# Two Mamba layers: GpSimd's products moved to slots 2, 7 and 12 of a block, the gates and some background steps one slot later

## The chip, the cores and the metric

The kernel runs on one core of one Trainium2 chip. The core's engines each work through their own list of instructions in order and wait for each other by semaphores: TensorE (PE, with PEld for its weight loads), VectorE (DVE), ScalarE (ACT), GpSimd (POOL) and SyncE (SP, which here issues the DMAs). The metric is the device time of one launch in microseconds (us). The kernel before takes 11773.98 us, the median of three runs (11769.27 to 11785.81).

## The reference, cut to what matters

Four images of 256 channels by 64 x 64 pixels go through four residual layers: two of gated recurrence with windowed attention, one Mamba layer, one grouped Mamba layer. The change is in the last two. Both hold the same selective scan, over 4096 tokens; the Mamba layer has 512 inner channels, the grouped one has four groups of 64 channels with 128 inner channels each:

```python
def step(h, inp):
    d_t, u_t, B_t, C_t = inp
    dA = jnp.exp(d_t[..., None] * A)
    h = dA * h + (d_t * u_t)[..., None] * B_t[:, None, :]
    y_t = jnp.einsum('bdn,bn->bd', h, C_t)
    return (h, y_t)
_, ys = jax.lax.scan(step, h0, xs)
y = ys.transpose(1, 0, 2) + u * D
y = y * jax.nn.silu(z)
```

The state has 16 columns n for each channel. `B` and `C` are rows per token that all channels share; `delta` (`d_t`) and `u` are per channel and token. In the grouped layer the result goes on through a layer norm, two dense layers with a gelu, a 1x1 convolution and a batch norm.

## The kernel before, in words

Each layer cuts the tokens into four chunks of 1024 (`k`), and each chunk into four blocks of 128 channels (in the grouped layer a block is a group; a chunk has two pairs `c`, and a pair has an even and an odd block). `scan_blocks` (L907 to L1072) runs all 16 blocks of a layer in one list of 256 slots: one slot is one state column n of one block, so a block has slots 0 to 15. In slot i:

- TensorE spreads row n of B over 128 partitions into a PSUM tile `pb` (`spread`, L949), VectorE multiplies it by `du` (delta times u; L1029), ScalarE computes `da` = exp(delta A) (`decay`, L961), VectorE scans (L1039).
- GpSimd multiplies the scanned `h` by the row of C, `cb`, which a DMA has spread (L925), giving `hc` (L1045). TensorE transposes `hc` and adds it up in `y` (`turn`, L977), one slot behind.
- Slots named in the argument `apart` do the product with B otherwise: a DMA spreads the row of B into `bb` (L931), GpSimd multiplies it by `du` (`product`, L935) two slots ahead of its scan, and VectorE only scans. There `da` is kept in the PSUM tile in place of `pb` and is called `dap`. The first slot of a layer is never apart.

The order of every engine is written out by hand in the loop:

```python
for i, (blk, n) in enumerate(slots):
    if not is_apart(i): nc.vector.tensor_tensor(pb[i], blk["du"], pb[i], ALU.mult)
    for step in blk["bg"].get(("between", n), ()): step()
    if i >= DS: gate(slots[i - DS][0], n)
    ...                       # VectorE's scan of slot i
    product(i + 2)
    ...                       # GpSimd's hc of slot i
    decay(i + 3); keep(i - 1); load_c(i + 3); load_b(i + 4)
    ...                       # the block before: end(); background steps of slot n
    spread(i + 2)
    ...                       # background steps of slot n + 0.5
    turn(i - 1); decay(i + 2, True)
```

`pb` and `dap` share two PSUM buffers (so slot i + 2 can be filled once scan i is done), `h`, `hc` have three buffers, `cb` four, `bb` one, `y` one. The block before is finished while the next one runs: in the slots of `ends` ScalarE copies `y` out (L995) and TensorE turns it back in two halves (L1001); in the slots of `gates` VectorE multiplies the two halves by the silu of z, ahead of that slot's scan (L988).

All other work is background: `put(block, slots, steps)` hangs the steps of the next chunk or pair onto slots. A step ("between", n) goes ahead of the scan of slot n, a step n behind the `hc` of slot n, a step n.5 behind the `spread`. The steps that this document follows: `norm` (position and add on GpSimd in the Mamba layer, mean L1103, center L1106, deviation L1117 to L1081, scale L1123 on GpSimd, affine L1130), `x_proj` (two projections whose results go by DMA to the tables of B and C, then the three bf16 parts of B, with the two `rest` products on GpSimd, L1206), `delta` (two projections, two additions on VectorE L1171, and `du` on GpSimd L1175), `mlp` (its scaling L1815 is on GpSimd), and `out` (an addition on GpSimd L1896 and a DMA out).

Of the kernel before, what the change touches and what calls it, by code (L numbers as in the profile page):

```python
# [28 lines left out]
NC = 1024  # L29
# [15 lines left out]
class Net:  # L45
# [1191 lines left out]
    def mamba_layer(self, x, bridge, pe_dram, w_in, w_cw, w_x, w_dt, w_out, v_dram):  # L1237
        tc, nc = self.tc, self.nc
        ND = 4
        with ExitStack() as ctx:  # L1240
            wp = ctx.enter_context(tc.tile_pool(name="m2_w", bufs=1, reuse_waits="tile"))
            work = ctx.enter_context(tc.tile_pool(name="m2_a", bufs=2, reuse_waits="tile"))
            loop = ctx.enter_context(tc.tile_pool(name="m2_b", bufs=2, reuse_waits="tile"))
            dram = ctx.enter_context(tc.tile_pool(name="m2_d", bufs=2, space=DRAM))
            psum = ctx.enter_context(tc.tile_pool(name="m2_p", bufs=2, space=PSUM))
            psb = ctx.enter_context(tc.tile_pool(name="m2_q", bufs=2, space=PSUM))
# [243 lines left out]
            for k in range(n_chunk):  # L1490
                more = k + 1 < n_chunk
                bg = [blk["bg"] for blk in chunks[k]["blocks"]]

                def put(d, where, steps):
                    for i, f in zip(where, steps):
                        bg[d].setdefault(i, []).append(f)

                def soft(d, places, steps):
                    p0, a0, p1, a1, du = places
                    put(d, (p0, ("between", a0), p1, ("between", a1), du), steps)  # L1500

                if k == 0:
                    put(0, (2, 3, 4, 5), [lambda d=d: diag_taps(d) for d in range(ND)])
                if k:
                    for i, where in enumerate(((3, 4, 5), (6, 7, 8), (9, 10, 11), (12, 13, 14))):
                        put(0, where, out_proj(k - 1, i // 2, i % 2))
                soft(0, (9, 11, 11, 13, 13), delta(k, 1))
                put(0, (14, 15), (in_z(k, 0, 0), in_z(k, 0, 1)))
                z1 = in_z(k, 1, 0), in_z(k, 1, 1)
                z3 = in_z(k, 3, 0), in_z(k, 3, 1)  # L1510
                put(1, (0, 1, 2, 4), (*z1, *z3))
                put(1, (1.5,), (silu((k, 0, "zs"), (k, 1, "zs")),))
                soft(1, (6, 8, 8, 11, 11), delta(k, 2))
                at = (6, 8, 8, 10, 10) if more else (5, 7, 7, 9, 9)
                soft(2, at, delta(k, 3))
                at = (10, 11) if more else (8, 9)
                put(2, at, (in_z(k, 2, 0), in_z(k, 2, 1)))
                if more:

                    if k == 0:  # L1520
                        put(0, (0,), (lambda: begin(1),))
                        put(0, (0, 0, 1, 3, 4, 5, 6, 7), self.later(lambda: norm(1, 0), 8))
                    h1 = self.later(lambda k=k: norm(k + 1, 1), 8)
                    if k:
                        put(0, (2, 4, 5, 7, ("between", 9), 13, 14, 15), h1)
                    else:
                        put(0, (7, 8, 9, 12, ("between", 14), 14, 15), h1[:7])
                        put(1, (1,), h1[7:])
                    if k + 2 < n_chunk:
                        put(3, (3,), (lambda k=k: begin(k + 2),))  # L1530
                        h0 = self.later(lambda k=k: norm(k + 2, 0), 8)
                        put(3, (4, 6, 7, 14, 15), h0[:5])
                        chunks[k + 1]["late"] = ((0, 1, 2), h0[5:])
                    if k:
                        put(0, *chunks[k]["late"])
                    u = all_u(k + 1)
                    put(1, (5, 7, 9, 10, 11, 12, 13, 14, 15), u[:9])
                    put(2, (0, 1, 5, 7, 9, 12, 13, 14, 15), u[9:18])
                    put(3, (0, 1, 2, 4, 5, 6), u[18:])
                    xs = x_proj(k + 1)  # L1540
                    put(2, (13,), (silu((k + 1, 0, "u"), (k + 1, 1, "u"), (k, 2, "zs"),
                                        (k, 3, "zs")),))
                    put(3, (7,), (silu((k + 1, 2, "u"), (k + 1, 3, "u")),))
                    put(3, (8, 8.5, 9, 9.5), xs)
                    soft(3, (10, 12, 11, 13, 13), delta(k + 1, 0))
                    put(3, (10, 11, 12, 13), xs[4:])
                else:
                    put(2, (13,), (silu((k, 2, "zs"), (k, 3, "zs")),))

                    sums, about, square, squares, early_squares = stats  # L1550

                    def square_into(i):
                        tag, bufs = ("pe", 1) if i % 2 else ("u", 5)
                        square(i, work.tile([P, NC], F32, tag=tag, name="cs_sq", bufs=bufs))

                    for i in range(6):
                        put(1 + (13 + i) // DS, ((13 + i) % DS,), (lambda i=i: sums(i),))
                        put(2 + (12 + i) // DS, ((12 + i) % DS,), (lambda i=i: square_into(i),))
                        put(2 + (13 + i) // DS, ((13 + i) % DS,), (lambda i=i: squares(i),))
                    put(2, (3,), (about,))  # L1560
                    put(3, (3,), (early_squares,))
                    for i in range(4):
                        at = (6 + 2 * i, 7 + 2 * i)
                        put(3, at, out_proj(k, i // 2, i % 2, ((0, 1, 2),)))
# [18 lines left out]
            def center(s):  # L1583
# [5 lines left out]
                )  # L1589

            self.scan_blocks(
                [blk for c in chunks for blk in c["blocks"]], loop, psum, psb, psy, (0, 5, 10),
                (1, 2, 4), (3, 5), (xs0[4:6], (), xs0[6:]),
                {1: [lambda: mean3(0)], 2: [lambda: center(0)], 4: [lambda: mean3(1)],
                 5: [lambda: center(1)]},
            )
# [52 lines left out]
    def grouped_mamba_layer(self, x, bridge, begun, ws_dram, outc_dram, v_dram, out_b, load):  # L1649
        tc, nc = self.tc, self.nc  # L1650
        w_in, w_cw, w_x, w_dt, w_out, w_f1, w_f2 = ws_dram
        with ExitStack() as ctx:
# [123 lines left out]
            def x_proj(k, q):  # L1776
                blk = chunks[k]["blocks"][q]

                def make():
                    blk["bct"] = work.tile([P, NC], F32, tag="bct", name="m3_bct", bufs=1)  # L1780
                    blk["parts"] = work.tile([P, NC], BF16, tag="parts", name="m3_parts")
                    blk["cd"] = dram.tile([2, DS, NC], F32, tag="cd", name="m3_cd")

                def project(ps, ss, part):
                    nc.tensor.matmul(ps, wx, blk["u"][:, ss], start=True, stop=True)

                return self.table_steps(blk, make, project, psum, 1)

            def delta(k, q):
                return self.delta_steps(chunks[k]["blocks"][q], wdt, work, psum)  # L1790
# [101 lines left out]
            def out(k, s, m, eng=nc.gpsimd):  # L1892
                def step():
                    t0 = k * NC + s
                    xs = x[:, m * T + t0 : m * T + t0 + NT]
                    eng.tensor_tensor(yo(k, s, m), xs, yo(k, s, m), ALU.add)  # L1896
                    nc.sync.dma_start(out_b[m * P : (m + 1) * P, t0 : t0 + NT], yo(k, s, m))

                return step
# [110 lines left out]
            for i, (k, c) in enumerate(pairs):  # L2010
                even, odd = chunks[k]["blocks"][2 * c : 2 * c + 2]

                def put(blk, where, steps):
                    for i, f in zip(where, steps):
                        blk["bg"].setdefault(i, []).append(f)

                def soft(blk, places, steps):
                    p0, a0, p1, a1, du = places
                    put(blk, (p0, ("between", a0), p1, ("between", a1), du), steps)
# [7 lines left out]
                if more:  # L2027
                    h0, h1 = (self.later(lambda k=k, s=s: norm(k + 1, s), 5) for s in range(2))
                    put(even, (0,), (lambda k=k: begin(k + 1),))
                    put(even, (0, ("between", 2), 4, 5, 6), h0)  # L2030
                    put(even, (14, 15), h1)
                    put(odd, (1, 2, 3), h1[2:])
                put(even, (4, 5, 9, 11, 12, 13) if i else (6, 7, 9, 11, 12, 13), x_proj(k, 2 * c + 1))
                if i:
                    m0, m1 = mlp(*pairs[i - 1], 0), mlp(*pairs[i - 1], 1)
                    put(even, (6, 7, 8, 10, 11, 11.5, 12.5, 13.5), m0)
# [6 lines left out]
                        late.append(((0, 0.5, 1.5, 2), m1[4:]))  # L2043
                    else:
                        put(odd, (5, 6, 6.5, 7.5, 8.5), m1[3:])
                soft(even, (7, 9, 8, 10, 10) if i else (9, 11, 10, 12, 12), delta(k, 2 * c + 1))
                also = [lambda k=k: out_silu(k - 1)] if c == 1 and k else []
                if i == 0:
                    put(even, (1, 2), [in_z(0, 0, s) for s in range(2)])
# [4 lines left out]
                    put(even, (12, 13, 14, 15), folds)  # L2054
                put(even, (3 if i else 5,), (silu(k, c, "zs", also),))
                if c == 1 and k:
                    put(even, (4, 5, 6, 7), [out(k - 1, *sm) for sm in outs])
                    put(even, (8,), [lambda k=k: load(slice((k - 1) * NC, k * NC))])
                if c == 0 and k:
                    put(odd, (8, 12, 15), [out_conv(k - 1, *sm) for sm in outs[:3]])  # L2060
                    late.append(((0,), [out_conv(k - 1, *outs[3])]))
# [6 lines left out]
                    soft(odd, (10, 12, 11, 13, 13), delta(nk, 2 * ncol))  # L2068
                    put(odd, (13, 14), [in_z(nk, ncol, s) for s in range(2)])
            self.scan_blocks(  # L2070
                [blk for c in chunks for blk in c["blocks"]], loop, psum, psb, psy, (0, 4, 8),
                (1, 2, 3), (3, 4), (xs0[2:4], (), xs0[4:]),
            )

            k, pair = n_chunk - 1, chunks[-1]["blocks"][2:]
# [160 lines left out]
```

## Time and profile before

| what | value |
|---|---|
| median of three runs | 11773.98 us |
| the profiled execution | 11766.22 us, span 11764.4 us |
| scan stages of the Mamba layer, four images | 927.3, 927.2, 925.7, 927.7 us |
| scan stages of the grouped layer, four images | 956.5, 955.6, 956.9, 954.5 us |
| the eight scan stages together | 7531.3 us, 64% of the span |
| VectorE busy in a scan stage | about 869 us (both layers) |
| GpSimd busy in a scan stage | about 799 us (Mamba), 852 us (grouped) |
| ScalarE busy in a scan stage | about 537 us (Mamba), 678 us (grouped) |
| TensorE busy in a scan stage | about 750 us (Mamba), 745 us (grouped), clock granted 0.94, 0.91 |

A scan stage is counted from the first scan's start to the last scan's end in the trace. The four images run alike, to within 2 us. Busy time is the sum of an engine's instructions; what is left of a stage is time in which that engine waited for something.

### The profile page before, as it was taken

The page shows a single profiled execution, that of the slowest core. Times are in us where ns is not written, and L with a number is a line of the kernel's source. Part 1 is how long each engine was busy: PE and PEld are TensorE (multiplying, and loading weights), DVE is VectorE, ACT ScalarE, POOL GpSimd, SP SyncE. Part 2 cuts the span into 40 slices and gives each one's busy share as a digit, 9 for nine tenths or more (in the row PEclk, how much of TensorE's full clock was granted, in tenths as well). Part 3 has the DMA queues.
Part 4 walks back from the last instruction along what each step waited for, and adds up shares of the span by engine and source line. Part 5 has one row for each costly group of instructions (what it writes and reads, how often), then busy time and mean ns, then how long its engine had stood idle before and what let it go on. Part 6 is the DMA issues. An engine that isn't in the chain of part 4 may idle for free. (4 is left out here: it accounts for less than half of the span.)

```text
span 11764.4 us, 192822 instructions
## 1 busy us (share of the span) xinstructions
PE 9808.9 (83%) x71200; PEld 5732.9 (49%) x71200; DVE 9739.8 (83%) x8290; ACT 7203.5 (61%) x13520; POOL 8779.1 (75%) x6054
## 2 busy tenths in 40 slices
PE   8997887777899788777799978877778997887787
PEld 4564444444466444444446644444444564444444
DVE  6677998898667799889866779988987678998898
ACT  4566555776456655577645665557764566555776
POOL 4666887898466688789846668878984666887897
PEclk9998998999999899899999999989999999998999
DMA  3344544454334454445423445544543344554454
GB/s 98 105 138 139 177 171 150 167 179 163 88 107 137 138 176 174 148 169 180 165 83 111 139 141 177 174 148 168 180 161 92 104 141 147 171 176 150 168 172 154
DMA packets 682477, 1742.10 MB, mean 148 GB/s; under 512 B 88880, under 2 KB 194880, under 8 KB 681280
## 3 DMA queue, kind: packets, MB, share of 16 engines
q1 hardware_dynamic: 676416, 1721.38, 44.5%
q8 instruction: 564, 9.24, 0.3%
q10 hardware_dynamic: 5120, 8.39, 0.3%
q14 instruction: 377, 3.09, 0.1%
HBM read 1601.49 MB, written 94.39 MB: 144 GB/s over the span
## 5 line engine op out<-in xcount | busy, mean ns | idle before, releaser
L1045 POOL TENSOR_TENSOR hc<-h,cb 128x1024 f32<-128x1024 f32 x2056 | 4810.6, 2351 | 792.1 <-DVE h L1039 403.6
L1039 DVE TENSOR_TENSOR_SCAN h<-da,m_state,pb 128x1024 f32<-128x1024 f32 x1248 | 2917.7, 2338 | 144.6 <-ACT m_state L966 17.8
L977 PE MATMUL y<-ident,hc 128*128 128x128 f32 x16384 | 2380.5, 293 | 518.9 <-POOL hc L1045 404.4
L977 PEld LDWEIGHTS y<-ident,hc 128*128 128x128 f32 x16384 | 2053.8, 151 | 1271.3 <-POOL hc L1045 691.8
L1029 DVE TENSOR_TENSOR pb<-du,pb 128x1024 f32<-128x1024 f32 x1672 | 2020.4, 1208 | 140.7 <-PE pb L949 134.7
L961 ACT ACTIVATE da<-delta,m_v 128x1024 f32<-128x1024 f32 x1672 | 1898.2, 1140 | 136.3 <-DVE h L1039 110.0
L949 PE MATMUL pb<-m_parts,pick 128*128 128x512 bf16 x3312 | 1076.3, 409 | 929.7 <-DVE h L1039 886.2
L603 POOL TENSOR_SCALAR pr<-pr,sm,zero 128x256 f32<-128x256 f32 x2048 | 1107.3, 556 | 375.2 <-DVE sm L600 371.0
L588 ACT ACTIVATE pr<-sc,mn 128x256 f32<-128x256 f32 x2048 | 953.0, 477 | 507.2 <-DVE sm L600 400.7
L949 PEld LDWEIGHTS <-pick 128*128 128x128 bf16 x3312 | 258.7, 101 | 1823.0 <-DVE h L1039 1196.6
L577 DVE TENSOR_REDUCE mn<-sc 128x4 f32<-128x1024 f32 x512 | 630.1, 1232 | 529.5 <-PE sc L565 529.5
L1039 DVE TENSOR_TENSOR_SCAN h<-da,pb 128x1024 f32<-128x1024 f32 x424 | 968.4, 2284 | 54.5 <-ACT m_state L966 11.3
L935 POOL TENSOR_TENSOR bb<-du,bb 128x1024 f32<-128x1024 f32 x376 | 888.2, 2362 | 127.4 <-DMA bb<-m_cd 113.3
L1039 DVE TENSOR_TENSOR_SCAN h<-dap,m_state,bb 128x1024 f32<-128x1024 f32 x288 | 673.5, 2338 | 95.0 <-POOL bb L935 67.8
L252 PE MATMUL conv_ps<-att_y,att_wb 128*128 128x512 f32 x1536 | 682.5, 594 | 0.0
L616 PE MATMUL pt_ps<-ident,pr 128*128 128x128 f32 x4096 | 638.0, 291 | 41.3 <-POOL pr L603 20.8
L961 ACT ACTIVATE dap<-delta,m_v 128x1024 f32<-128x1024 f32 x376 | 418.6, 1113 | 338.5 <-DVE h L1039 323.3
L565 PE MATMUL sc<-kv,q_swap 32*64 32x128 f32 x8192 | 592.8, 282 | 18.9 <-DMA kv<-kv_dram 8.0
L565 PE MATMUL sc<-kv,att_y 32*64 32x128 f32 x7168 | 573.3, 282 | 23.6 <-DMA kv<-kv_dram 20.5
L616 PEld LDWEIGHTS pt_ps<-ident,pr 128*128 128x128 f32 x4096 | 458.8, 146 | 169.6 <-POOL pr L603 111.9
L290 DVE SCALAR_TENSOR_TENSOR lp<-vimg,att_v,lp 128x512 f32<-128x512 f32 x672 | 507.7, 755 | 30.4 <-DVE lp L290 0.5
L565 PEld LDWEIGHTS sc<-kv,att_y 32*64 32x64 f32 x7168 | 424.9, 136 | 154.2 <-ACT pr L588 72.6
(303 smaller groups left out, 17725.3 us busy)
## 6 DMA issues: line engine op xcount, KB each, us to landing
cb<-m_cd SPq DMA_DIRECT2D x2048, 512.0 KB, 3.8
kv<-kv_dram SPq DMA_DIRECT2D x1984, 128.0 KB, 2.8
bb<-m_cd SPq DMA_DIRECT2D x376, 512.0 KB, 4.9
kv_dram<-kst SPq DMA_DIRECT2D x128, 256.0 KB, 3.6
kv_dram<-vn SPq DMA_DIRECT2D x128, 256.0 KB, 4.1
q_swap<-att_y SPq DMA_DIRECT2D x96, 256.0 KB, 4.3
m_pe<-in_pe_dram SPq DMA_DIRECT2D x32, 512.0 KB, 4.3
out_dram<-yo SPq DMA_DIRECT2D x64, 256.0 KB, 2.4
```

Of the source, the lines that this page charges most:

```text
L252: nc.tensor.matmul(ps, w[:, k, w0 + m * P : w0 + (m + 1) * P], src[:, k], start=(k == 0), stop=(k == 1),)
L565: nc.tensor.matmul(sc[h][b * 64 : b * 64 + 64, r, w, m, :], (own(sj, m) if r == b else swap[sj % 2][:, m])[rows, 2 * a + w], kv[i, w][rows ...
L588: nc.scalar.activation(t[:, g].rearrange("p j r t -> p r j t"), sc[h][:, :, g // 2, g % 2, :].rearrange("p r (j t) -> p r j t", j=2), AF.E ...
L603: nc.gpsimd.tensor_scalar(t[:, g], t[:, g], s[:, g : g + 1], self.zero, ALU.mult, ALU.add)
L616: nc.tensor.transpose(pt[h][j][:, g, :], t[:, g, j].rearrange("p r t -> p (r t)"), self.ident,)
L935: nc.gpsimd.tensor_tensor(pb[i], slots[i][0]["du"], pb[i], ALU.mult)
L949: nc.tensor.matmul(pb[i][:, ss], self.pick[:, n : n + 1].to_broadcast([P, P]), blk["parts"][:, ss], start=True, stop=True,)
L961: nc.scalar.activation(da[i], blk["delta"], AF.Exp, scale=blk["a"](n))
L977: nc.tensor.matmul(blk["y"][:, ss], t[:, ss], self.ident, is_transpose=True, start=(n == 0 and ss.start % NT == 0), stop=(n == DS - 1 and ...
L1029: nc.vector.tensor_tensor(pb[i], blk["du"], pb[i], ALU.mult)
L1039: nc.vector.tensor_tensor_scan(h[i][:, ss], da[i][:, ss], pb[i][:, ss], state, ALU.mult, ALU.add)
L1045: nc.gpsimd.tensor_tensor(hc[i][:, ss], h[i][:, ss], cb[i][:, ss], ALU.mult)
```

## The change

In `scan_blocks`'s arguments, `apart` becomes (2, 7, 12) in both layers (it was (0, 5, 10) in the Mamba layer and (0, 4, 8) in the grouped one), and both gates of a block move one slot later. In the Mamba layer three steps of the second norm of a chunk move one slot later (add, mean, center). In the grouped layer the even block's norm of the next chunk's first half, the first two steps of `x_proj`, the second addition of `delta` with `du`, the four additions to the output with their DMAs, and the load of the next image's columns move one slot later.

```diff
 mamba_layer
-                        put(0, (2, 4, 5, 7, ("between", 9), 13, 14, 15), h1)
+                        put(0, (2, 4, 6, 8, ("between", 10), 13, 14, 15), h1)
...
-                ... loop, psum, psb, psy, (0, 5, 10), (1, 2, 4), (3, 5), ...
+                ... loop, psum, psb, psy, (2, 7, 12), (1, 2, 4), (4, 6), ...
 grouped_mamba_layer
-                    put(even, (0, ("between", 2), 4, 5, 6), h0)
+                    put(even, (1, ("between", 3), 4, 6, 7), h0)
...
-                put(even, (4, 5, 9, 11, 12, 13) if i else (6, 7, 9, 11, 12, 13), x_proj(k, 2 * c + 1))
+                put(even, (5, 6, 9, 11, 12, 13) if i else (6, 7, 9, 11, 12, 13), x_proj(k, 2 * c + 1))
...
-                soft(even, (7, 9, 8, 10, 10) if i else (9, 11, 10, 12, 12), delta(k, 2 * c + 1))
+                soft(even, (7, 9, 8, 11, 11) if i else (9, 11, 10, 12, 12), delta(k, 2 * c + 1))
...
-                    put(even, (4, 5, 6, 7), [out(k - 1, *sm) for sm in outs])
-                    put(even, (8,), [lambda k=k: load(slice((k - 1) * NC, k * NC))])
+                    put(even, (5, 6, 7, 8), [out(k - 1, *sm) for sm in outs])
+                    put(even, (9,), [lambda k=k: load(slice((k - 1) * NC, k * NC))])
...
-                ... loop, psum, psb, psy, (0, 4, 8), (1, 2, 3), (3, 4), ...
+                ... loop, psum, psb, psy, (2, 7, 12), (1, 2, 3), (4, 5), ...
```

## The prediction

> **What bounds the kernel now.** I read the page's groups first, then VectorE's waits, then its timeline slot by slot.
>
> ```profile
> span 11764.4 us, 192822 instructions
> ...
> L1045 POOL TENSOR_TENSOR hc<-h,cb 128x1024 f32<-128x1024 f32 x2056 | 4810.6, 2351 | 792.1 <-DVE h L1039 403.6
> L1039 DVE TENSOR_TENSOR_SCAN h<-da,m_state,pb 128x1024 f32<-128x1024 f32 x1248 | 2917.7, 2338 | 144.6 <-ACT m_state L966 17.8
> ...
> L1029 DVE TENSOR_TENSOR pb<-du,pb 128x1024 f32<-128x1024 f32 x1672 | 2020.4, 1208 | 140.7 <-PE pb L949 134.7
> ...
> L935 POOL TENSOR_TENSOR bb<-du,bb 128x1024 f32<-128x1024 f32 x376 | 888.2, 2362 | 127.4 <-DMA bb<-m_cd 113.3
> ```
>
> The last number before the bar is the count, then busy us and mean ns, then the idle time ahead. A normal slot costs VectorE 1.21 + 2.34, 3.6 us with the gaps; an apart slot 2.26. A block needs 13 x 3.6 + 3 x 2.26 = 53.6 us plus gates, additions and centers, while GpSimd's fixed part is 19 x 2.36 = 44.8 us. VectorE is busy about 869 us in each stage of 926 to 957, so it sets the pace, and only its waits can be won:
>
> ```profile
> DVE pb L1029 <- PE pb L949: 134.7, 97, 3.1
> DVE m_zs L988 <- PE fin_ps L1001: 97.0, 50, 4.4
> DVE h L1039 <- POOL bb L935: 78.2, 77, 2.4
> ...
> DVE h L1039 <- ACT dap L961: 43.7, 30, 2.2
> ...
> DVE h L1039 <- ACT m_state L966: 29.6, 26, 1.9
> ...
> DVE m_zs L988 <- ACT m_zs L1388: 26.6, 13, 2.3
> ```
>
> That is us in total, times, longest: 410 us, 3.5% of the span. Gate waits are 124 us, waits of an apart scan 122 us. By slot they sit at the head of blocks. The timeline of VectorE at slots 2 to 5 of the Mamba layer's fifth block:
>
> ```profile
> 1230.57 1.21 DVE L1029 TENSOR_TENSOR pb<-du,pb 128x1024 f32<-128x1024 f32 x1
> 1233.52 0.69 DVE L988 TENSOR_TENSOR m_zs<-fin_ps,m_zs 128x512 f32<-128x512 f32 x1 [1.75 <-PE fin_ps L1001]
> ```
>
> and GpSimd's where a grouped even block (the seventh) meets the odd one:
>
> ```profile
> 2374.43 2.12 POOL L1206 TENSOR_TENSOR m_bct<-m_bct,m_parts 64x1024 f32<-64x1024 f32 x1
> 2376.52 4.67 POOL L1045 TENSOR_TENSOR hc<-h,cb 128x1024 f32<-128x1024 f32 x2
> 2381.15 2.13 POOL L1206 TENSOR_TENSOR m_parts<-m_bct,m_parts 32x1024 bf16<-32x1024 f32 x1
> 2383.25 2.34 POOL L935 TENSOR_TENSOR bb<-du,bb 128x1024 f32<-128x1024 f32 x1
> 2385.56 4.67 POOL L1045 TENSOR_TENSOR hc<-h,cb 128x1024 f32<-128x1024 f32 x2
> ```
>
> Slot 0's product stands at 2383.25, ahead of slot 14's hc. So hc, y, its copy, fin_ps and the gate (wait 2.27 us there) all come 2.34 us later: the two families of waits have one source.
>
> **The change, part by part.** I write E_n for the end of slot n's scan.
>
> *Count.* Slot 0 of a layer couldn't be apart, slot 2 can: 8 more products on GpSimd, 8 fewer on VectorE, 8 x 1.21 = 10 us less. SP issues 8 more bb loads of 512 KB. The Trainium skill (GPSIMD Engine Reference, Engine selection) says to keep elementwise work off GpSimd, where a two-input operation is about twice as slow. The rows agree on the price (2.36 against 1.21); by the rule 8 such moves lose 8 x 1.15 = 9 us, by the rows, with VectorE as the bound and GpSimd idle 11 to 14% of a stage, they win 10. I take the rows.
>
> *Mamba layer, heads of blocks.* First block of chunks 1 and 2: VectorE's waits above its floor are 0.9 at slot 0 (bb), 2.4 at slot 2 (pb), 1.7 and 0.3 at the gates, 5.3 us. After the change product(2) is behind hc(15), so hc(14) ends 2.3 us sooner. TensorE then does the norm's deviation (3.9 us) from 26.4 on a clock that starts with the old tail at slot 9; ScalarE's square root ends at 32.3 to 33 and, behind it in its queue, dap of slot 2 at 33.4 to 34.2. Scan 2 would want it at 32 to 33: a new wait of about 1 to 1.8 us. The gate, a slot later, finds fin_ps done. Against it, at slot 12 of the block before, the addition to delta and dap both stand behind ScalarE's exp chain: about 1.5 us more there. Net, end of slot 5 against end of slot 5, -3 us. For chunk 3, without that norm, -0.3.
> Second blocks: the gate waits 2.6 us (1.7 in chunks 0 and 3) for the silu of z that ScalarE does in slot 1.5; a slot is 3.6 us, so all of it goes, with 0.8 to 1.3 of other waits in chunks 0 and 3: -2.3, -2.5, -2.5, -2.8. The skill (ScalarE: Activation LUTs, What ACT_TABLE_LOAD costs) puts a change of tables at 2.66 us with its drain. Here the load's row is 1.28 us and the next activation starts 0.01 later. By the page the silu would end 1.4 us later than I count and some 0.4 of the wait would stay; the trace is used.
> Fourth blocks: slot 0's dap waits 2.0 to 2.2 us behind the silu step of slot 13 (four silus and two loads, 6.6 us). Slot 0 is a normal slot now and its da is issued ahead of that step: -2.1, three times.
> First block of chunk 0: product(7) and dap(7) stand behind the norm's deviation in slot 5: I bound it by 0 and +2.5 and take +1.5.
> Sum per image: chunk 0 -6, chunk 1 -7.5, chunk 2 -5, chunk 3 -3: -21 us.
>
> *Grouped layer.* Won: gate waits of 2.2 us (first blocks) and 2.3 to 3.1 (fourth), slot 0's waits for bb (0.5 to 1.5 in every block, 2.3 once), and slot 2 of third blocks (2.2 to 2.9: TensorE has out_conv and the mean between; the mean and center are moved to slots 1 and 3). Lost: in an even block slots 10 to 13 now carry product(12), one L1815, du and both L1206 beside four hc: 2.36 + 1.28 + 2.36 + 4.25 + 9.44 = 19.7 us where VectorE takes 13.5. In a first block, from E_9 = 0, GpSimd's queue ends at: hc(9) 2.4, product(12) 4.8, hc(10) 7.1, L1815 8.4, hc(11) 10.8, L1206 12.9, du 15.3, hc(12) 17.6, hc(13) 20.0, L1206 22.1, hc(14) 24.5, hc(15) 26.9, product(2) 29.2; VectorE's scans 10 to 15, unhindered, at 3.6, 7.6 (an addition), 9.9 (apart), 13.5, 17.1, 20.6. The second L1206 must precede TensorE's spread of the next slot 0, which wasn't needed when that slot was apart. VectorE wants it at 20.6 and gets it at 22.75: +2.1 at the odd block's slot 0, and behind that spread in TensorE's queue stand the turn of slot 13, spread of slot 1 and the mlp's products, so dap of slot 2 (behind gelu's chain) is 0.7 late too. Worst is the third block, with four out additions (5.1 us) and a norm scale (2.0) in slots 5 to 8: I get hc(10) 6.0 us late, scan 12 waiting 2.0 for its product, scan 15 waiting 2.2 for a free h buffer, and slot 0 of the fourth block 2.8 for its spread: 7.0, against 6 to 7 of waits there before. Its output DMAs and the cd tables shift with their steps on SP; the bb loads now find their buffer free (27 us of POOL's waits for them per image go). Odd blocks: slot 12's dap behind ScalarE's delta chain costs 1.1 to 1.8, the wait at slot 6 for TensorE (1.2 to 2.3) goes.
> Adding these schedules, end of slot to end of slot: -2.2 us for a chunk's first pair, -2.1 for its second, about three full chunks' worth: -13 us per image. Both are small differences between sums of 7 to 10 us, with single margins under 1 us. Bounds: -20 (no new wait) and +18 (all new waits, none of the old ones at slots 2 and 6 gone). I take half, -6.5.
>
> Sum: 4 x (-21 - 6.5) - 10 = -120 us. Against the profiled execution, 11766.2, that is 11646; the median lies 8 us higher, so 11654, rounded to 11650 (-1.05%).
>
> The gates in the tail of a layer change places with a center (1.2 us) once per image; the attention layers (36% of the span) are untouched. Both at nothing.
>
> **Rivals.** (1) GpSimd becomes the bound in the grouped layer: slower. Place: slots 10 to 15 of even blocks. Price: 7.0 + 1.2 at the second pair, 2.1 + 0.7 + 1.1 at the first, 12 us a chunk or 193 us over 16 chunks if TensorE's waits at slots 2 and 6 stay as they are; less 94 of the Mamba layer: +100, 11870. It decides once the new waits exceed the old ones by 6 us a chunk. For it: hc is 5 us late there already, in third blocks. Against: POOL's work in a third block, 61 us, was the same before, and its lag is carried into odd blocks that have 6 us to spare.
> (2) The grouped layer gives back what the Mamba layer gains, up to 60 of 94 us: 11720 to 11790.
> (3) Nothing: each gate wait turns into a pb or dap wait one slot on, since TensorE (81% busy) was the real limit: 11750 to 11797. Against: after the head of a block VectorE runs ten slots in a row without waiting.
> (4) The grouped layer's full -13 or better, as mamba's: below 11580.
>
> **How the numbers follow.** Likeliest, 0.58: 11580 to 11720, about 11650. Rival 4: 0.10; rival 2: 0.13, of which 0.09 is faster by over 0.2%; rival 3: 0.05; rival 1: 0.14. About 0.2% (24 us) is what a measurement of this kernel can tell from no change. Faster 0.58 + 0.10 + 0.09 = 0.77, same 0.04 + 0.05 = 0.09, slower 0.14. A range of 11560 to 11800 leaves out about 0.06 below and 0.13 above.
>
> **What would show it.** Right: gate waits (L988) from 124 us to under 40, "h <- POOL bb" and "h <- ACT dap" together under 122, Mamba stages near 905 us, products x384. In the grouped layer stages of 940 to 955, new pb waits at slot 0 of odd blocks of about 2 us, GpSimd without gaps from slot 5 to 15 of third blocks. Wrong: grouped stages above 975 (rival 1), or Mamba stages still above 920 (rival 3).

## The result, and the profile after

| what | before | after |
|---|---|---|
| median | 11774.28 us (18 runs) | 11798.36 us (18 runs) |
| ratio, with its 95% interval | | 1.002 [1.0013, 1.0027] |
| span of the profiled execution | 11764.4 us | 11796.3 us |
| Mamba scan stages, mean of four images | 927.0 us | 925.5 us |
| grouped scan stages, mean of four images | 955.9 us | 963.1 us |
| the rest of the span (no line of it changed) | 4233.1 us | 4241.6 us |

The kernel became 24 us slower, not 120 us faster. Four Mamba stages won 6 us and four grouped stages lost 29. The rest of the span lies between 4227 and 4252 us over the fourteen kernels of this study, so its 8.5 us are not put down to the change.

The groups of the page, in the order in which they were shown before:

```profile
span 11796.3 us, 193082 instructions
...
L1045 POOL TENSOR_TENSOR hc<-h,cb 128x1024 f32<-128x1024 f32 x2056 | 4809.8, 2349 | 917.8 <-DVE h L1039 359.8
L1039 DVE TENSOR_TENSOR_SCAN h<-da,m_state,pb 128x1024 f32<-128x1024 f32 x1248 | 2917.0, 2337 | 145.7 <-ACT m_state L966 26.0
...
L1029 DVE TENSOR_TENSOR pb<-du,pb 128x1024 f32<-128x1024 f32 x1664 | 2012.6, 1209 | 212.5 <-PE pb L949 206.9
...
L935 POOL TENSOR_TENSOR bb<-du,bb 128x1024 f32<-128x1024 f32 x384 | 907.0, 2362 | 19.4 <-DMA bb<-m_cd 19.1
```

The counts moved by 8 each way at unchanged prices, and GpSimd hardly waits for the row of B any more (127.4 us of idle time ahead of its products before, 19.4 now). But VectorE's products now stand idle for 212.5 us where it was 140.7. Its waits, in us in total, times, longest:

```profile
DVE pb L1029 <- PE pb L949: 206.9, 173, 3.8
...
DVE h L1039 <- ACT dap L961: 93.0, 68, 3.5
...
DVE h L1039 <- ACT m_state L966: 41.5, 43, 1.8
...
DVE m_zs L988 <- PE fin_ps L1001: 17.7, 7, 4.4
DVE h L1039 <- POOL bb L935: 13.4, 7, 2.7
```

The waits that the change aimed at are gone: gates 124 us before, 18 now; `bb` 78 before, 13 now. The spread of B (135 to 207), `dap` (44 to 93) and the state copy (30 to 42) came up in their place, and the additions to delta wait 92 us for ScalarE where it was 46. (The 18 us of gate waits that are left all lie behind the last scan of a layer, outside the scan stages.) TensorE's waits hold lines that the kernel before does not have at all; by far the largest is the last of these:

```profile
PE y L977 <- POOL hc L1045: 212.6, 222, 4.2
PE pb L949 <- POOL m_parts L1206: 117.0, 44, 5.4
...
PE u_ps L1732 <- DVE m_zs L988: 53.6, 28, 2.4
```

`u_ps` is the grouped layer's projection for the next pair, four steps of the odd blocks (slots 4 to 7). Twenty-eight is one for each of the seven odd blocks of an image that have a next pair.

To see where the time went, I summed for every block the time between the end of one scan and the start of the next that VectorE spent on no instruction. Over the sixteen blocks of a layer, after against before, as a mean of the four images: in the Mamba layer -0.8 us. In the grouped layer the even blocks won 12.4 us and the odd blocks lost 19.1: the loss is in one kind of block.

### The profile page after: what moved, and what is told of

Its sections match the earlier page's. It is cut to its first block, busy times and chain, and to the rows that moved or that the text cites. A ratio compares the mean times of both kernels' runs of the same rounds, so it can differ in the third digit from the quotient of the medians.

```text
span 11796.3 us, 193082 instructions
## 1 busy us (share of the span) xinstructions
PE 9907.0 (84%) x71184; PEld 5803.1 (49%) x71184; DVE 9727.1 (82%) x8282; ACT 7184.1 (61%) x13520; POOL 8788.2 (74%) x6062
## 5 line engine op out<-in xcount | busy, mean ns | idle before, releaser
L977 PE MATMUL y<-ident,hc 128*128 128x128 f32 x16384 | 2398.6, 295 | 330.9 <-POOL hc L1045 212.6
L977 PEld LDWEIGHTS y<-ident,hc 128*128 128x128 f32 x16384 | 2088.2, 153 | 1095.5 <-POOL hc L1045 437.8
L1029 DVE TENSOR_TENSOR pb<-du,pb 128x1024 f32<-128x1024 f32 x1664 | 2012.6, 1209 | 212.5 <-PE pb L949 206.9
L935 POOL TENSOR_TENSOR bb<-du,bb 128x1024 f32<-128x1024 f32 x384 | 907.0, 2362 | 19.4 <-DMA bb<-m_cd 19.1
```

Source lines behind the costliest of these rows:

```text
L935: nc.gpsimd.tensor_tensor(pb[i], slots[i][0]["du"], pb[i], ALU.mult)
L977: nc.tensor.matmul(blk["y"][:, ss], t[:, ss], self.ident, is_transpose=True, start=(n == 0 and ss.start % NT == 0), stop=(n == DS - 1 and ...
```

## Experiments

Every ratio is to the kernel before, measured beside it. Stages are means of four images.

| run | median us | ratio [95% interval] | Mamba stage | grouped stage |
|---|---|---|---|---|
| m_only | 11778.43 | 1.0005 [0.9996, 1.0014] | 926.7 | 956.4 |
| g_gates_back | 11738.1 | 0.9971 [0.9958, 0.9983] | 925.8 | 949.2 |
| g_u_later | 11724.5 | 0.9959 [0.9944, 0.9973] | 926.9 | 945.8 |
| g_xproj_early | 11872.31 | 1.0081 [1.0064, 1.0097] | 927.0 | 980.3 |
| gates_only | 11763.45 | 0.9996 [0.9987, 1.0005] | 926.8 | 954.7 |
| apart_only | 11716.25 | 0.9962 [0.9948, 0.9976] | 927.2 | 944.4 |
| u_scale_later | 11752.64 | 0.999 [0.9981, 0.9998] | 912.7 | 966.4 |
| norm_back | 11734.73 | 0.9975 [0.9964, 0.9985] | 926.6 | 947.7 |
| mamba_u_old | 11754.97 | 0.9984 [0.9976, 0.9991] | 923.3 | 954.7 |
| both_parts | 11673.1 | 0.9912 [0.9899, 0.9926] | 912.1 | 943.4 |
| both_affine | 11660.97 | 0.9895 [0.9879, 0.9911] | 913.0 | 942.2 |
| apart_gates | 11817.05 | 1.0032 [1.0019, 1.0045] | 927.1 | 966.8 |

### Which layer

Only the Mamba half of the change on the kernel before:

```diff
-  put(0, (2, 4, 5, 7, ("between", 9), 13, 14, 15), h1)
+  put(0, (2, 4, 6, 8, ("between", 10), 13, 14, 15), h1)
-  (0, 5, 10), (1, 2, 4), (3, 5)      # Mamba layer: apart, ends, gates
+  (2, 7, 12), (1, 2, 4), (4, 6)
```

> The Mamba layer's part of the change alone (products in slots 2, 7 and 12, gates at 4 and 6, the norm's three steps a slot later); the grouped layer as before. Theory (the loss is the grouped layer's): the Mamba scan stages stay at the 925.5 us that they have after the whole change (927.0 before), the grouped ones go back to 956, so 4 x 1.5 = 6 us faster than before, 11768 us. Rival (the Mamba part pushes cost into other stages): no faster than before, 11774 or more.

The Mamba half does nothing (1.0005, the interval holds 1). The loss belongs to the grouped half, and what the Mamba half was to win is missing too. These are two questions.

### The grouped layer: which buffer a gate frees

Two runs on the changed kernel. The first puts only the grouped gates back; the second keeps them and moves the work that meets them.

```diff
 g_gates_back
-  (2, 7, 12), (1, 2, 3), (4, 5)      # grouped layer
+  (2, 7, 12), (1, 2, 3), (3, 4)
 g_u_later
-  put(odd, (4, 5, 6, 7), all_u(nk, ncol))
+  put(odd, (5, 6, 7, 8), all_u(nk, ncol))
-  put(odd, (7,), (silu(nk, ncol, "u"),))
+  put(odd, (8,), (silu(nk, ncol, "u"),))
-  put(odd, (8, 12, 15), [out_conv(...) ...])
+  put(odd, (8.5, 12, 15), [out_conv(...) ...])
```

> The whole change, with the grouped layer's gates back at slots 3 and 4. Theory (a fin_ps tile holds one of the two small PSUM buffers until its gate has read it, and the odd blocks' u_ps, from slot 4, waits for that buffer): the 54 us of TensorE's waits of u_ps for VectorE's gate go, the waits of VectorE at slots 6 and 7 of odd blocks fall by some 15 to 20 us per image, gate waits come back at 4 to 8 us per image; grouped stages from 963 to about 951, total about 11750. Rival (GpSimd's queue behind the new products is the cost): nothing at slots 6 and 7 changes, the gate waits come back in full, grouped stages 963 to 975.

> The whole change, with the grouped layer's input projection and convolution (u_ps) of the next pair in slots 5 to 8 of the odd block instead of 4 to 7, its silu in slot 8, and the first out_conv of that block behind the spread of slot 8; the gates stay at 4 and 5. Theory (PSUM buffer held by the gate): u_ps no longer waits for the gate (54 us to under 10), the waits of slots 6 and 7 fall by half, some waits move to slots 10 to 12; grouped stages about 955. Rival (TensorE is simply too full in those slots, whichever buffer it waits for): the same waits a slot later, 960 or more.

Both hold, and by more than was expected: 13.9 us a stage come back in the first, 17.3 in the second, and the line `u_ps <- DVE m_zs` is in neither trace. The waits at slots 6 and 7 of odd blocks are gone in both. What takes their place is smaller: waits of 1.2 to 1.9 us for the gate in slot 3 of most of these blocks in the first run, and of up to 3.2 us at slots 11 and 12 in the second. The mechanism can be read in the timeline of the changed kernel, in the sixth block of a grouped stage (an odd one), slots 4 to 7: TensorE's rows first, then VectorE's, then ScalarE's. The columns are start and duration in us, and in brackets the idle time ahead with what ended it.

```profile
2277.37 1.12 PE L1732 MATMUL u_ps<-m_xn,m_wi 64*128 64x512 f32 x2
2280.63 3.75 PE L1732 MATMUL u_ps<-m_xn,m_wi 64*128 64x512 f32 x6 [2.14 <-DVE m_zs L988]
2284.31 1.04 PE L949 MATMUL pb<-m_parts,pick 128*128 128x512 bf16 x2
...
2275.84 0.68 DVE L988 TENSOR_TENSOR m_zs<-fin_ps,m_zs 128x512 f32<-128x512 f32 x1
...
2279.81 0.68 DVE L988 TENSOR_TENSOR m_zs<-fin_ps,m_zs 128x512 f32<-128x512 f32 x1
...
2285.39 1.23 DVE L1029 TENSOR_TENSOR pb<-du,pb 128x1024 f32<-128x1024 f32 x1 [2.65 <-PE pb L949]
...
2291.44 2.35 DVE L1039 TENSOR_TENSOR_SCAN h<-dap,m_state,bb 128x1024 f32<-128x1024 f32 x1 [2.34 <-ACT dap L961]
...
2289.06 1.26 ACT L1739 ACTIVATE m_u<-u_ps,m_v 128x512 f32<-128x512 f32 x2 [10.05 <-PE u_ps L1732]
2290.22 1.12 ACT L961 ACTIVATE dap<-delta,m_v 128x1024 f32<-128x1024 f32 x1
```

`fin_ps` and `u_ps` are both tiles of the one `psum` pool with the tag "mm", which has two buffers. The gate is the last reader of `fin_ps`; a gate in slot 5 keeps its buffer until 2280.49. The first `u_ps` tile takes the other buffer at 2277.37, the second has to wait for this gate. Behind it in TensorE's queue stands the spread of slot 6, which VectorE waits for (2.65 us), and `u_ps` itself is copied out late, with `dap` of slot 7 behind that copy in ScalarE's queue (2.34 us). The wait is charged twice over, since TensorE worked at half speed for some us behind it (its granted clock is 1.00 from 2276.9 to 2280.3 and 0.50 from 2280.3 to 2287.1; see the last section). The group of `u_ps` shows it, 64 us more for the same 896 matmuls than in the kernel before. Before, then after:

```profile
L1732 PE MATMUL u_ps<-m_xn,m_wi 64*128 64x512 f32 x896 | 230.4, 633 | 0.0
...
L1732 PE MATMUL u_ps<-m_xn,m_wi 64*128 64x512 f32 x896 | 294.5, 672 | 53.6 <-DVE m_zs L988 53.6
```

and with `u_ps` a slot later:

```profile
L1732 PE MATMUL u_ps<-m_xn,m_wi 64*128 64x512 f32 x896 | 231.2, 613 | 0.0
```

### The grouped layer: gates, apart slots, and the two together

Three runs on the kernel before, the grouped layer's arguments alone:

```diff
-  (0, 4, 8),  (1, 2, 3), (3, 4)
+  (0, 4, 8),  (1, 2, 3), (4, 5)      # gates_only
+  (2, 7, 12), (1, 2, 3), (3, 4)      # apart_only
+  (2, 7, 12), (1, 2, 3), (4, 5)      # apart_gates
```

> The kernel before with one edit: the grouped layer's gates at slots 4 and 5 instead of 3 and 4. Theory (fin_ps holds a small PSUM buffer until its gate): the gate waits of that layer (59 us) go, but u_ps waits for the gate by some 50 us in total and VectorE's pb waits at slot 6 of odd blocks grow; no gain: grouped stages 956 to 962, total 11775 to 11800. Rival (a gate a slot later is free, the loss of the whole change lies with the products): 948 or less, 11740.

> The kernel before with one edit: the grouped layer's products on GpSimd in slots 2, 7 and 12 instead of 0, 4 and 8; gates at 3 and 4 and all background steps as before. Theory (the new slots are good in themselves, the gates undid it): grouped stages near the 949 of the whole change with its gates back, total about 11745. Rival (the shift of norm, x_proj, du and out is what makes room for slot 12's product): GpSimd late in even blocks, 957 or more, 11778 or more.

> The kernel before with the grouped layer's apart slots 2, 7, 12 and gates at 4 and 5 and nothing else; the two edits were run one by one before. Theory: neither the gates alone nor the apart slots alone delay the u_ps tiles; with slot 4 a normal slot (3.6 us with its product) the second gate stands a product and a scan later than with slot 4 apart, and TensorE, ahead by then, waits for the buffer that it frees. Waits of u_ps for the gate come back (about 50 us of TensorE in all), waits of 2 to 3 us at slots 6 and 7 of odd blocks, grouped stages of about 957 to 960 against 944.5, the time 11765 to 11780. Rival: the clash needs the moved norm, x_proj and additions as well: stages of 943 to 947, the time about 11710.

What was expected of gates_only did not happen: `u_ps` waits 1.4 us in all for the gate there, not some 50, so that its time stayed as it was is right by the number alone. The apart slots alone won more than I had expected (944.4 us a stage against about 949). The pair went as told, and lost more (966.8 against 957 to 960). Against 955.9 us a stage the gates alone give -1.2, the apart slots alone -11.5, and the two together +10.9: they cost 24 us a stage on top of their sum. Why the gates are harmless alone is in the timeline of the kernel with the gates alone, at the same place, VectorE's rows and then TensorE's:

```profile
2270.13 2.34 DVE L1039 TENSOR_TENSOR_SCAN h<-dap,m_state,bb 128x1024 f32<-128x1024 f32 x1
...
2273.50 0.68 DVE L988 TENSOR_TENSOR m_zs<-fin_ps,m_zs 128x512 f32<-128x512 f32 x1
...
2271.77 1.90 PE L977 MATMUL y<-ident,hc 128*128 128x128 f32 x8 [1.71 <-POOL hc L1045]
2273.46 1.91 PE L1009 MATMUL y<-ident,m_u 128*128 128x128 f32 x8
2275.30 1.13 PE L1732 MATMUL u_ps<-m_xn,m_wi 64*128 64x512 f32 x4
```

There slot 4 is apart. Its product on GpSimd goes ahead of `hc` of slot 2 and makes it late (TensorE waits 1.71 us for it), so TensorE starts `u_ps` at 2275.30, behind the gate's end at 2274.18. With slots 2, 7 and 12 apart TensorE is early at slot 4, as it was meant to be, and the gate is later, since VectorE has slot 4's product to do first: the gate of slot 5 ends 5.68 us behind the scan of slot 3 in the changed kernel, 4.55 us here. So TensorE runs into the gate. With both edits, and nothing else changed, the wait is back:

```profile
PE u_ps L1732 <- DVE m_zs L988: 60.4, 28, 2.4
```

The other moves of the change (norm, x_proj, delta, additions) are not the cause. With the old gates they cost 4.8 us a stage (g_gates_back 949.2 against apart_only 944.4). With the new ones the changed kernel has 963.1 against 966.8, but its four stages (961.0 to 966.1) and those of apart_gates (962.5 to 971.8) overlap, so that they help there isn't shown.

### The grouped layer: the two other new waits

The second `rest` product (L1206) ahead of slot 0 of an odd block is late, as the prediction said: TensorE waits for it, and VectorE for TensorE, in the changed kernel's same block at its slot 0.

```profile
2257.14 2.11 POOL L1206 TENSOR_TENSOR m_parts<-m_bct,m_parts 32x1024 bf16<-32x1024 f32 x1
...
2259.30 0.59 PE L949 MATMUL pb<-m_parts,pick 128*128 128x512 bf16 x2 [2.24 <-POOL m_parts L1206]
...
2259.93 1.23 DVE L1029 TENSOR_TENSOR pb<-du,pb 128x1024 f32<-128x1024 f32 x1 [1.50 <-PE pb L949]
```

I tried to take this wait away by doing the last three steps of x_proj a slot earlier (on the changed kernel):

```diff
-  put(even, (5, 6, 9, 11, 12, 13) if i else ..., x_proj(k, 2 * c + 1))
+  put(even, (5, 6, 9, 10, 11, 12) if i else ..., x_proj(k, 2 * c + 1))
```

> The whole change, with the last three steps of the even block's x_proj, both L1206 among them, in slots 10 to 12 instead of 11 to 13. Theory (TensorE's spread for the odd block's slot 0 waits for the second L1206, which GpSimd reaches late): VectorE's waits at slot 0 of odd blocks, 1.7 to 1.9 and 0.6 to 3.2 us, fall under 0.5, that is about 10 us per image; grouped stages from 963 to about 953, total about 11760. Rival (GpSimd is full from slot 7 to 15, so the order within it doesn't matter): the waits move to scans 12 to 15, stages stay at 960 or more.

I missed. The waits at slot 0 do go (0.1 to 0.2 us; the first pair, which the edit leaves alone, keeps a wait of 2.3 for `cw_ps`), but the stages are 17 us longer: slot 14 of the even blocks waits 4.2 to 6.6 us. The rival named that place, with another reason. ScalarE's `parts` step now waits for GpSimd's product with a table load and the gelus behind it; TensorE waits for the gelus' buffers with the spread of slot 14 behind. ScalarE's rows, then TensorE's, then VectorE's, at slots 12 to 14 of the fifth block:

```profile
2255.07 1.06 ACT L1203 ACTIVATE m_parts<-m_bct 64x1024 bf16<-64x1024 f32 x1 [1.94 <-POOL m_bct L1206]
2256.14 1.28 ACT L1828 ACT_TABLE_LOAD   x1
2257.44 1.27 ACT L1828 ACTIVATE hid<-f_ps,m_f1b 128x512 f32<-128x512 f32 x2
...
2258.18 2.65 PE L1821 MATMUL f_ps<-m_sq,m_wf 64*128 64x512 f32 x4 [3.68 <-ACT hid L1828]
...
2263.62 1.23 DVE L1029 TENSOR_TENSOR pb<-du,pb 128x1024 f32<-128x1024 f32 x1 [3.93 <-PE pb L949]
```

The second new wait, 2.2 to 2.8 us at slot 9 of third blocks, I took for an effect of the norm that was moved, so I put its last two steps back (on g_u_later):

```diff
-  put(even, (1, ("between", 3), 4, 6, 7), h0)
+  put(even, (1, ("between", 3), 4, 5, 6), h0)
```

> The kernel of the run with u_ps in slots 5 to 8, with the even block's norm scale and affine back at slots 5 and 6 (they are at 6 and 7 after the change). Theory (in third blocks the affine waits for GpSimd's scale with delta's exp chain behind it in ScalarE's queue): VectorE's waits at slots 9 and 10 of third blocks, 2.7 and 1.0 us, fall under 1 together; grouped stages from 945.7 to about 938, total about 11695. Rival (GpSimd is full there in any order): the wait moves to scans 5 to 8 or to the outputs, stages stay above 943.

It gains nothing: slot 9 still waits 2.0 to 3.4 us, only at another instruction (the product, for TensorE's spread, and no longer the addition to delta, for ScalarE). apart_only, with the old norm, has that wait too (3.0 to 3.4), so it comes with the new apart slots. My reading is that GpSimd's product for slot 7 goes ahead of the norm's scale, and ScalarE's affine waits for the scale with other work behind it; both_affine, below, tests the part of the affine.

### The Mamba layer: ScalarE's order at the head of a block

In second blocks the gate waited 1.7 to 2.6 us before. After, the gate doesn't wait, and the product of the same slot waits 2.5 us (3.5 in chunk 0, nothing in chunk 3). The changed kernel's timeline, sixth block of a Mamba stage, ScalarE's rows, TensorE's, then VectorE's:

```profile
1289.07 1.07 ACT L995 ACTIVATE du<-y 128x512 f32<-128x512 f32 x2
...
1290.24 1.77 PE L977 MATMUL y<-ident,hc 128*128 128x128 f32 x8 [2.37 <-issue]
1291.80 1.06 PE L1001 MATMUL fin_ps<-ident,du 128*128 128x128 f32 x4
1292.66 2.48 PE L1375 MATMUL z_ps<-m_xn,m_wz 128*128 128x512 f32 x4
1294.97 0.59 PE L949 MATMUL pb<-m_parts,pick 128*128 128x512 bf16 x2
...
1295.61 1.23 DVE L1029 TENSOR_TENSOR pb<-du,pb 128x1024 f32<-128x1024 f32 x1 [2.64 <-PE pb L949]
```

`y` has one buffer, so the turn of slot 0 has to wait until ScalarE has copied the old `y` out (the profile names no releaser for that wait; the copy ends 0.10 us ahead of the turn). Behind that turn stand `fin_ps`, the projection for z, and the spread of slot 4. The same place in the kernel before, TensorE's rows, then VectorE's:

```profile
1290.79 1.06 PE L977 MATMUL y<-ident,hc 128*128 128x128 f32 x8 [1.28 <-issue]
...
1293.85 0.59 PE L949 MATMUL pb<-m_parts,pick 128*128 128x512 bf16 x2
...
1293.09 0.69 DVE L988 TENSOR_TENSOR m_zs<-fin_ps,m_zs 128x512 f32<-128x512 f32 x1 [2.32 <-ACT m_zs L1388]
1293.70 2.34 DVE L1039 TENSOR_TENSOR_SCAN h<-da,m_state,pb 128x1024 f32<-128x1024 f32 x1
```

This spread ended at 1294.44, with VectorE held by the gate until 1293.78 and by a scan until 1296.04: it was nearly as late, and hidden.

The slower clock is in this wait too. The turn of slot 0 started sooner after the change (1290.24 against 1290.79), and yet the spread ended later (1295.56 against 1294.44): the same work took TensorE 5.32 us where it was 3.65. Ahead of it TensorE paused for 2.37 us, 1.28 before, and its granted clock from 1290.2 to 1295.0 is 0.64, before it is 1.00. So 1.7 of the 2.6 us are the clock; without it about 1.0 us would be left, an estimate from these rows. All four images have the pause of 2.37 us in the second blocks of chunks 1 and 2, with slow transposes behind it.

The copy stands in ScalarE's queue behind `u`'s scaling by D (1.14 us), which TensorE needs only in slot 3 (`turn_u`). So the scaling was put in slot 2, behind the copy; in the first run in both layers on the changed kernel, in the second in the Mamba layer of the kernel before:

```diff
-  if n == 1:
+  if n == 2:
       nc.scalar.activation(blk["u"], blk["u"], AF.Identity, scale=blk["d"])
```

> The whole change, with ScalarE's scaling of u by D (1.13 us, both layers) in slot 2 instead of slot 1, so that it stands behind the copy of y and not ahead of it. Theory (the new pb waits at slot 4 come from the chain copy of y, turn of slot 0 into the single y buffer, fin_ps, spread of slot 4): in the Mamba layer's second blocks that wait falls from 2.5 to 1.4 us, in the fourth from 1.0 to about 0; Mamba stages from 925.5 to about 920, grouped ones about 1 less, total about 11770. Rival (TensorE's own work between, z_ps above all, sets it): no wait changes by more than 0.3, 11795 or more.

> The kernel before with one edit: in the Mamba layers the scaling of u by D (ScalarE, 1.14 us) is issued in slot 2 of a block instead of slot 1; apart slots 0, 5, 10 and gates 3, 5 stay. Theory: what the Mamba half of the change lacked was only ScalarE's order at the head of a block. With the old gates the copy of y and the silu of z come 1.1 us sooner, so the gate of the second blocks (1.7 to 2.6 us) waits about 1.1 us less, and the other heads lose little: Mamba stages 922 to 925, the time 11750 to 11760, far less than the 13 us a stage that the same edit gave with the changed gates and apart slots. Rival: the scaling alone is the limit and the gates and apart slots of the Mamba layer do nothing: stages of about 913, the time about 11715.

Mamba stages go from 925.5 to 912.7 us with the changed gates and apart slots, and only from 927.0 to 923.3 with the old ones. So gates and apart slots alone are worth 0.3 us (m_only), the scaling alone 3.7, and all together 14.3. What one hid the other needed. The first run won more than expected (912.7 against about 920), because the wait fell from 2.6 to 0.3 us in chunks 1 and 2 and not to 1.4: TensorE's pause is 1.55 us now, the clock stays at 1.00, and the work from the turn of slot 0 to the spread takes 3.65 us again. In chunk 0 the wait is still 2.7. The second run met its number (923.3) but not its reason: the gate of second blocks waits 1.7 to 2.7 us as before, and what went are the gate waits of 1.7 us in the first blocks of chunks 1 and 2. The spread of slot 4 now ends in time, with VectorE not waiting; the same place in u_scale_later:

```profile
1286.91 1.06 PE L977 MATMUL y<-ident,hc 128*128 128x128 f32 x8 [1.55 <-issue]
...
1288.25 1.88 PE L1375 MATMUL z_ps<-m_xn,m_wz 128*128 128x512 f32 x4
1289.97 0.59 PE L949 MATMUL pb<-m_parts,pick 128*128 128x512 bf16 x2
...
1290.60 1.23 DVE L1029 TENSOR_TENSOR pb<-du,pb 128x1024 f32<-128x1024 f32 x1
```

The grouped stages of that run are 966.4 us (961.7 to 970.8), where about 1 us less than 963.1 was expected. No gain is to be seen there, so in that layer the scaling was left in slot 1.

### Putting it together

both_parts is the kernel before with m_only's edits, the scaling in slot 2 of the Mamba layer alone, and apart_only's edit. both_affine moves one step of it:

```diff
-  put(even, (0, ("between", 2), 4, 5, 6), h0)
+  put(even, (0, ("between", 2), 4, 5, 7), h0)
```

> The Mamba half of the change with the scaling of u in slot 2 (Mamba layers only), and of the grouped half the apart slots 2, 7, 12 alone (gates 3 and 4 and every other step as before). Theory: the layers don't touch each other, so the gains of the two runs that had them add: Mamba stages about 913, grouped about 944.5, 4 x (927 - 913 + 956 - 944.5) = 102 us under the kernel before, about 11670. Rival: they share something and give part of it back: 11700 or more.

> The same as both_parts with the affine step of the grouped layer's even norm in slot 7 instead of 6 of third blocks. With slot 7 apart GpSimd does the norm's scale one product later, and ScalarE's affine waits for it with the copies of the mlp's m_ps behind it, so TensorE's spread of slot 9 comes 3 us late there. Theory: the copies go ahead of it and the wait of 3.0 us at slot 9, three times an image, goes to 1 or less: grouped stages about 938, 20 to 25 us under both_parts. Rival: the affine then stands ahead of delta's exponentials or the square root instead, and the wait only changes its name: within 8 us of both_parts.

The gains add: 11673.1 us, where 11670 was expected. The waits of VectorE in both_parts, to set against those of before and after:

```profile
DVE pb L1029 <- PE pb L949: 119.0, 112, 3.5
...
DVE m_zs L988 <- PE fin_ps L1001: 65.0, 52, 4.4
DVE h L1039 <- ACT m_state L966: 25.6, 31, 1.8
DVE h L1039 <- ACT dap L961: 25.0, 34, 1.9
...
DVE h L1039 <- POOL bb L935: 17.2, 10, 2.7
```

All five are smaller than before; the additions to delta (L1171) rose from 46 to 77 us. Gate waits of 65 us are left, 47 of them in the grouped stages, where they are cheaper than what takes their place (apart_only against apart_gates). both_affine did to slot 9 what it was to do (2.3 to 3.0 us became 0.3 to 0.8 in the first three chunks), but slots 10 and 12 together took up 2.3 and 1.4 us of it in the second and third chunk; its stages are 1.2 us shorter, not 5 to 6, and its interval overlaps that of both_parts. That it is the better of the two isn't shown. Both beat the kernel before and the changed one.

## Why the prediction was wrong, point by point

**What bounds the kernel** was right: VectorE sets the pace of the scan stages and only its waits can be won. Each version that won time here did it by fewer waits of VectorE.

**Count.** Right: x384 and x1664 at 2.36 and 1.21 us, 7.8 us less of VectorE's products.

**The Mamba layer, -21 us an image; measured -1.5.** The step that failed is the one on second blocks, "a slot is 3.6 us, so all of it goes". It followed the silu of z, which does come in time, and not the spread that stands behind the same copy of `y`, and it took TensorE's work at its old speed. From block end to block end second blocks moved by +0.7, -0.6, -0.6, -3.6 us in the four chunks (means of the four images), where -2.3 to -2.8 was predicted. Only in chunk 3 did all of it go: no norm of a next chunk stands in ScalarE's queue ahead of the copy there (two affine steps of 0.8 us), and TensorE's pause is 0.72 us. That is rival 3's sign, in this layer, with its sentence "VectorE runs ten slots in a row without waiting" as the wrong argument against it: the spread was late at slot 4 all the time, behind a gate that was later. Its reason, TensorE as the real limit, is not borne out: moving one step of ScalarE took the wait away.

Two more steps failed. Fourth blocks were to win 2.1 us each at slot 0 and moved by +1.5, +0.8 and +1.1, by size the largest miss of the layer. The wait at slot 0 is still 1.5 to 1.8, now for the state copy behind the same silu step of ScalarE, so naming `dap` alone was too narrow, and slot 4 waits 1.0 to 1.4 for its spread, as in second blocks. The first block of chunk 0 lost 4.8 us beside the product that it saved, where I took 1.5 of a bound of 2.5; the waits are at slots 2, 5 and 12, not at slot 7. The first blocks of chunks 1 and 2, from slot 5 to slot 5, won 3.3 and 1.1 of the 3 predicted. Slot 12 of fourth blocks lost 1.6, as said.

**The grouped layer, -6.5 us an image; measured +7.2.** The list of wins was right: even blocks won 12.4 us an image. The list of losses lacked the largest. The failed step is "the wait at slot 6 for TensorE (1.2 to 2.3) goes", together with gates costed only by their own waits: I asked what a later gate waits for, and not what waits for a later gate. Slots 6 and 7 of odd blocks wait 2.1 to 5.2 us together (means of the four images), where slot 6 of second blocks waited 1.2 to 2.5 and fourth blocks not at all. The bound of +18 that I gave the layer ("none of the old ones at slots 2 and 6 gone") covered it in size by luck; the cause is another. The step on slot 0 of odd blocks had the right mechanism: 2.1 predicted and 1.7 to 1.9 measured in second blocks, 2.8 predicted and 1.3 to 3.2 measured in fourth ones, both in the later three chunks. (The 2.4 of chunk 0's second block is another wait, for the convolution's `cw_ps`, which was not predicted.) In third blocks, the product and `h` buffer waits of 2.0 and 2.2 us did not come as told; a wait of 2.2 to 2.8 us at slot 9 for delta did, behind the product for slot 7, which I had not followed into ScalarE's queue.

**The rivals.** Rival 1 (GpSimd as the bound) gave the right sign with the wrong mechanism: taking away the gates' move, which gives GpSimd no less to do, turned the loss into a gain (0.9971). Rival 2 is excluded because the Mamba layer had no gain to give back. The limit set for rival 4 did not follow from its own terms: 4 x (-21 - 13) - 10 is -146 us, which is about 11630 and not below 11580.

**What would show it.** Gate waits under 40 and `bb` with `dap` under 122 both came out "right" (18 and 106) while the kernel lost time. The two stage lengths were the test that counted. The Mamba one (925.5) said rival 3 as it was written; the grouped one (963.1) lay between the 955 set for right and the 975 set for rival 1.

## What to carry to other kernels

Before moving a consumer later, ask which buffer it frees and who takes that buffer next: here two PSUM buffers were shared by the gates' input and the next projection, and the price of a later gate stood at another line than the gate. A wait on the pacing engine can hide a second one of the same size on the next slot; follow the engine that is waited for to the end of its queue, not only to the instruction that is named. And edits of an order by hand are not additive: run each alone and the pair, since here one pair cost 24 us a stage more than its parts and another won 10 us more.

## What the runs showed of the hardware

TensorE works at half speed for a while behind a stretch in which it had little to do, and one wait of about 2 us can make such a stretch: from 1287.0 to 1290.4 in the changed kernel, with the pause of 2.37 us, it was busy for 1.0 of 3.4 us. In the trace of the kernel before, its granted clock is 1.0 or 0.5, and every record of it but the last has a length that is a whole multiple of 3.41 us. Cut into stretches of 3.41 us, the trace has 183 at full clock in which TensorE was busy for less than 40%, and all 183 were followed by one at half clock; of the 2531 that were over 60% busy it was 19. In between it went either way (61 of 268). Back to full it went, but for one case, only behind stretches that were over 75% busy. After the change it is 189 of 189 and 16 of 2483.

The speed of the work agrees. In the trace of the kernel before, eight transposes (L977) that follow other work within 0.2 us take 1.04 us (median of 1660 groups), behind a gap of 1.5 to 2.0 us 1.09 (44 groups, 19 of them over 1.6), and behind one of 2.0 to 2.5 us 1.97 (27 groups, 21 of them over 1.6). In the rows above six matmuls of `u_ps` took 3.75 us behind the wait of 2.14, or 1.05 us each in the records where 0.59 is the median, and the transposes after them were still slow 4.5 us after the wait. So the waits of 53.6 us came with 64 us of slower matmuls. The Trainium skill (TensorE: Matmul & The Clock Gate, Part 1) describes a clock that falls to half behind an idle window of about 3.4 us; a pause of 2.1 us was enough in these traces. The mean granted clock of the whole kernel hardly shows it: 0.934 before, 0.930 after.
